# Building the down projection's compact weights in their final layout, and leaving the last batch's outermost two moment sums to TensorE

## The chip, the cores and the metric

The kernel runs on one NeuronCore of a Trainium2 chip. The metric is the device time of one execution in microseconds (us), as a median of several executions; lower is better.

## What is computed

The input `x` has four batches of 512 tokens by 512 features. It is normalised (layer norm without gain), and two branches work on the normalised `xn`: causal attention with 16 heads of width 32 and an ALiBi bias, and a gated feed-forward block whose three weight matrices are not given as matrices but as lists of control points of a cubic (Catmull-Rom) spline.

```python
xn = layernorm(x)
w_gate, w_up = spline(gate_cp).reshape(2048, 512), spline(up_cp).reshape(2048, 512)
w_down = spline(down_cp).reshape(512, 2048)
inter = silu(xn @ w_gate.T) * (xn @ w_up.T)
out = x + attention(xn) + inter @ w_down.T
# spline: sample t lies between control points 1 and 2 of four neighbours p0..p3, at fraction f;
# its weight is a cubic in f with coefficients made of p0..p3
```

One control point covers about 129 samples, so a row of a weight matrix (512 or 2048 samples) hangs on few control points. All data are float32.

## The kernel before, in words

**Attention** is cut into 64 units: batch b, group of four heads, tile of 128 queries. Unit n computes the scores of its tile on TensorE (L847), adds the bias and finds the row extreme on VectorE (L860), takes the exponential on ScalarE (L876), the reciprocal of the sum on VectorE (L889) and the product with it on GpSimd (L891). Three units later TensorE turns the probabilities by products with an identity matrix (L904), and the PSUM result is copied out by ScalarE (L909) or VectorE (L907). Every fourth unit multiplies by the values (L918). Between these steps each unit has a list `items[n]`: projections to q, k, v (L789, L820), the output projection of an earlier batch (L459), sums called moments (L487), loads. Loads and stores are all issued by one engine, SyncE (SP), in program order. The order of every engine's instructions is that of the program text, since `in_order` ties each instruction to the one before it on its engine. So an engine that waits holds back all that stands behind.

The turned tiles, the projections and the moments share one PSUM pool, `ps_m`, with three buffers named `mm`; a new tile can be written only when the copy out of the third tile before it is done.

**Making the weights.** While attention runs, VectorE also makes the feed-forward weights from control points, in small steps taken from a queue called `weights`. Each unit has a budget (2.4, 2.4, 1.2, 2.4 by n modulo 4, less 0.6 for each other small step), spent half in the middle and half at the end of the unit; each step has a cost and the queue is drained until the half is used up. First come the steps for gate and up (`row_weight_steps`, L612 and L615, 128x1024 elements an instruction, tables loaded into the tile `feat[0]` that the feed-forward block needs only later). Behind them comes `down_steps`:

- GpSimd clears the tile `wd` (L636).
- For each of four row groups r and each of 20 control points c, VectorE adds `table[r, c] * point[r, c]` to the columns of `wd` that this point can touch (L652, 80 instructions, 0.6 of the budget each). The point is one number a partition. Two points share a load of `tab` from HBM (L642, two buffers, 40 loads).
- In this form the 128 partitions are output rows. The feed-forward products need the strips the other way round, so TensorE turns `wd` by products with the identity (L668: nine strips of values for each r; L683: the moments), into `ps_m`, and ScalarE copies the result to `dRM` (L675, L684). `dRM` holds `dR`, the values of 9 x 128, and `dM`, the moments of 4 x 128.

**Feed-forward.** For each batch, gate and up products (L1072), Silu (L1087), their product (L1094), and down in two parts: the values (L1168) and the moments. For these, sums of 512-wide rows are formed per eighth e (L1119), copied, and added up from both sides, step by step, by VectorE (L1149, L1150); the results `u[0]` to `u[7]` enter a last product with `dM` (L1183). `down_moments` runs rows r = 3, 2, 1, 0; row 0 takes the outermost sums `u[7]` and `u[0]`, which are the last to be added. Then VectorE adds the residual (L1188) and SP stores the rows (L1189). For the last batch this chain ends the program.

Of the kernel before, what the change touches and what calls it, by code (L numbers as in the profile page):

```python
# [12 lines left out]
F32 = mybir.dt.float32  # L13
# [5 lines left out]
P = 128  # L19
# [25 lines left out]
ND = 64  # L45
NE = 8
NX = 9 + 4
NW, NW4 = 11, 4
NST = NW4 + 1

LINKS = [(0, 0), (2, 1), (1, 0), (2, 2), (1, 1), (3, 2), (4, 3), (3, 3)]
# [195 lines left out]
def down_tables(groups, eighth, alone, order):  # L247
# [75 lines left out]
    rows = np.stack([np.concatenate([groups[NE - 1 - r], groups[r]]) for r in range(NB)])  # L323
    table, ranges = [], []
    for c in range(NCD):
        a = parts[rows, c]
        hit = np.nonzero(a.any(axis=(0, 1, 2)))[0]
        lo, hi = int(hit[0]), int(hit[-1]) + 1
        ranges.append((lo, hi))
        table.append(a[..., lo:hi].reshape(NB, P, -1))  # L330
    return basis, np.concatenate(table, axis=2), ranges, points[rows], rows, homes

# [9 lines left out]
def single(a):  # L342
# [5 lines left out]
_coef, _stretch, ROW_POINTS = row_tables(ORDER)  # L348
_basis, _down, DOWN_RANGES, DOWN_POINTS, _rows, ALONE = down_tables(
    _groups, _eighth, _alone, KEPT  # L350
)
HORDER = _rows.reshape(-1)
# [23 lines left out]
def block_kernel(  # L376
# [45 lines left out]
    basist = keep.tile([P, NRT, ND], F32, name="basist")  # L422
    dpt = keep.tile([P, NB, NCD], F32, name="dpt")
    stretcht = keep.tile([P, len(LINKS), NRT * 4], F32, name="stretcht")
# [17 lines left out]
    dist = wp.tile([P, S], F32, name="dist")  # L442

    wd = wp.tile([P, NB * S], F32, name="wd")
    wdr = wd[:, : NB * NX * Q32].rearrange("p (r t x) -> p r t x", r=NB, x=Q32)
    ctxT = {}
# [79 lines left out]
    with ExitStack() as att:  # L526
        spl = att.enter_context(tc.tile_pool(name="spl", bufs=2))
        attw = att.enter_context(tc.tile_pool(name="attw", bufs=1))
# [26 lines left out]
        load_w("k", Wkp, attw)  # L555
        nc.sync.dma_start(out=dpt, in_=downpts)
        nc.sync.dma_start(out=stretcht, in_=stretch)
# [69 lines left out]

        offsets = np.cumsum([0] + [NX * (hi - lo) for lo, hi in DOWN_RANGES])
        PER = 2
        widest = int(max(offsets[c + PER] - offsets[c] for c in range(0, NCD, PER)))  # L630

        def down_steps():
            tabs = {}

            def clear():
                nc.gpsimd.memset(wd, 0.0)  # L636

            def load(r, c):
                def go():
                    lo, hi = int(offsets[c]), int(offsets[c + PER])  # L640
                    tabs[r, c] = spl.tile([P, widest], F32, name="tab")
                    nc.sync.dma_start(out=tabs[r, c][:, : hi - lo], in_=downtab[r, :, lo:hi])  # L642

                return go

            def term(r, c):
                def go():
                    tab = tabs[r, c - c % PER]
                    at = int(offsets[c] - offsets[c - c % PER])
                    lo, hi = DOWN_RANGES[c]  # L650
                    w = wdr[:, r, :, lo:hi]
                    nc.vector.scalar_tensor_tensor(  # L652
                        w,
                        tab[:, at : at + NX * (hi - lo)].rearrange("p (t x) -> p t x", t=NX),
                        dpt[:, r, c : c + 1],
                        w,
                        ALU.mult,
                        ALU.add,
                    )

                return go

            def turn_values(pairs):
                def go():
                    ps = ps_m.tile([P, NB, P], F32, name="mm")
                    for k, a in enumerate(pairs):
                        for r in range(NB):
                            nc.tensor.matmul(  # L668
                                ps[r * Q32 : (r + 1) * Q32, k, :],
                                lhsT=wdr[:, r, a],  # L670
                                rhs=ident,
                                start=True,
                                stop=True,
                            )
                    nc.scalar.copy(dR[:, pairs[0] : pairs[-1] + 1], ps[:, : len(pairs)])  # L675

                return go

            def turn_moments():
                ps = ps_m.tile([P, NB, P], F32, name="mm")  # L680
                for r in range(NB):
                    m = wdr[:, r, NRT // 2 + 1 :].rearrange("p t x -> p (t x)")
                    nc.tensor.matmul(ps[:, r, :], lhsT=m, rhs=ident, start=True, stop=True)  # L683
                nc.scalar.copy(dM, ps)  # L684

            loads = [(r, c) for r in range(NB) for c in range(0, NCD, PER)]
            steps = [(0.0, clear), (0.0, load(*loads[0])), (0.0, load(*loads[1]))]
            for n, (r, c0) in enumerate(loads):
                steps += [(0.6, term(r, c)) for c in range(c0, c0 + PER)]
                if n + 2 < len(loads):  # L690
                    steps.append((0.0, load(*loads[n + 2])))
            steps += [(1.0, turn_values(range(a, min(a + NB, 9)))) for a in range(0, 9, NB)]
            return steps + [(1.0, turn_moments)]


# [384 lines left out]

    around = {}
    acts, inner, own, sums, res = {}, {}, {}, {}, {}
# [27 lines left out]
    def inner_moments(b, tiles, pool, tag):  # L1110
# [65 lines left out]
    def down_moments(b):  # L1176
# [3 lines left out]
        for r in reversed(range(NB)):  # L1180
            for half, e in ((0, NE - 1 - r), (1, r)):
                cols = slice(half * ND, (half + 1) * ND)
                nc.tensor.matmul(  # L1183
                    sums[b][r][cols, :], lhsT=dM[:, r, cols], rhs=u[e], start=False, stop=True
                )
        for r in reversed(range(NB)):
# [100 lines left out]
```

## Time and profile before

| | before |
|---|---|
| median of 3 runs | 579.06 us (576.9 to 579.31) |
| profiled execution | 578.99 us, span from first to last instruction 576.9 us |
| TensorE busy | 564.1 us (98% of the span) |
| VectorE busy | 373.0 us (65%) |
| ScalarE busy | 296.9 us (51%) |
| GpSimd busy | 184.1 us (32%) |
| mean granted TensorE clock | 0.998 |
| DMA | 69.44 MB, mean 120 GB/s |

The span is what the trace covers; the time of the execution contains 2.1 us more around it. Line numbers (L652) are those of the kernel before. "PE" is TensorE's matmuls, "PEld" its weight loads, DVE is VectorE, ACT is ScalarE, POOL is GpSimd, SP is SyncE and SPq its queue of DMA issues. The trace shows each float32 matmul as two instructions (two passes).

### The profile page before, as it was taken

The numbers are of one execution on the slowest core, as the hardware profiler recorded it, in microseconds if no ns is written. First come the engines' busy times: TensorE is split into PE (matmuls) and PEld (weight loads), VectorE is DVE, ScalarE is ACT, GpSimd is POOL, SyncE is SP. The second block draws the span as 40 slices with busy tenths as digits, with TensorE's granted clock in tenths as the row PEclk, the third lists the DMA queues.
The fourth block names the chain that finished last, engine by engine and source line by source line (L and its number), as shares of the span: only waits on it lengthen the run. The fifth ranks groups of instructions, "written<-read, shape, count | busy, mean of one in ns | idle before, by whom it ended". The sixth has DMA issues, their size and how long they took to land.

```text
span 576.9 us, 11461 instructions
## 1 busy us (share of the span) xinstructions
PE 564.1 (98%) x4088; PEld 279.0 (48%) x4088; DVE 373.0 (65%) x1047; ACT 296.9 (51%) x786; POOL 184.1 (32%) x333
## 2 busy tenths in 40 slices
PE   7999999999999999999999999999999999999996
PEld 5645555444445555454555555555535333343342
DVE  6169988877687777768675444556244673854737
ACT  2457666554456665645655576677514512623322
POOL 2034525334232424233243242443124133122310
PEclk9999999999999999999999999999999999999999
DMA  8932246312422623432241004602445576774334
GB/s 310 337 70 74 73 148 219 95 25 60 152 81 73 212 69 106 114 122 65 68 142 46 2 1 97 124 1 84 137 129 175 107 175 197 135 203 171 112 149 159
DMA packets 36216, 69.44 MB, mean 120 GB/s; under 512 B 5984, under 2 KB 9568, under 8 KB 35648
## 3 DMA queue, kind: packets, MB, share of 16 engines
q1 hardware_dynamic: 36160, 68.72, 41.4%
q8 instruction: 32, 0.52, 0.4%
q14 instruction: 24, 0.20, 0.1%
HBM read 44.06 MB, written 15.29 MB: 103 GB/s over the span
## 4 chain that ended last, share of the span: by engine, by line
PE 76%; DMA 7%; DVE 7%; ACT 5%; SPq 3%; issue 1%; POOL 0%; DVEq 0%; POOLq 0%
PE mm L789 18%; PE mm L904 11%; PE mm L820 10%; PE s L847 6%; PE mm L459 6%; PE g L1072 6%; PE c L918 4%; PE o L1168 3%; ACT p L876 3%; PE o L459 3%; DMA feat<-samples 2%; PE o L1119 2%; PE mm L487 2%; DVE p L860 2%; PE g L1119 1%; PE o L1183 1%
## 5 line engine op out<-in xcount | busy, mean ns | idle before, releaser
L891 POOL TENSOR_SCALAR p<-p,inv 128x128 f32<-128x128 f32 (+3 forms) x256 | 140.2, 567 | 261.0 <-DVE inv L889 217.8
L876 ACT ACTIVATE p<-p,low 128x128 f32<-128x128 f32 (+3 forms) x256 | 140.7, 553 | 48.8 <-DVE low L860 48.5
L860 DVE CUSTOM_DVE_ANT_0 p<-s,dist 128x128 f32<-128x128 f32 (+3 forms) x256 | 109.1, 482 | 31.7 <-PE s L847 31.3
L904 PEld LDWEIGHTS mm<-ident,p 128*128 128x128 f32 x640 | 71.1, 141 | 40.6 <-issue 26.5
L904 PE MATMUL mm<-ident,p 128*128 128x128 f32 x640 | 89.2, 278 | 1.2 <-ACT pT L909 0.7
L909 ACT COPY pT<-mm 128x512 f32<-128x512 f32 x96 | 55.2, 580 | 53.4 <-PE mm L904 53.0
L1095 POOL COPY made<-inner 128x512 f32<-128x512 f32 x64 | 38.8, 633 | 109.6 <-DVE inner L1094 84.2
L1087 ACT ACTIVATE act<-g 128x512 f32<-128x512 f32 x64 | 33.3, 603 | 62.5 <-PE g L1072 62.5
L1072 PE MATMUL g<-feat,wT 32*128 32x512 f32 x432 | 59.6, 612 | 0.8 <-DMA feat<-moments 0.6
L820 PE MATMUL mm<-wv,xnT 128*128 128x512 f32 x128 | 58.3, 597 | 1.6 <-DMA wv<-in_Wvp_dram 1.0
L789 PE MATMUL mm<-xnT,wk 128*128 128x512 f32 (+1 forms) x136 | 59.3, 579 | 0.2 <-ACT xnT L774 0.2
L789 PE MATMUL mm<-xnT,wq 128*128 128x512 f32 (+1 forms) x136 | 58.0, 569 | 0.3 <-ACT pT L909 0.2
L847 PE MATMUL s<-kT,qT 32*128 32x512 f32 (+3 forms) x512 | 51.3, 468 | 0.3
L1094 DVE TENSOR_TENSOR inner<-g,act 128x512 f32<-128x512 f32 x44 | 27.3, 684 | 33.5 <-issue 10.1
L876 ACT ACTIVATION_READ_ACCUMULATOR p<-p,low 128x1 f32 x256 | 48.5, 189 | 0.0
L907 DVE COPY pT<-mm 128x512 f32<-128x512 f32 x64 | 43.6, 686 | 4.8 <-PE mm L904 4.2
L652 DVE SCALAR_TENSOR_TENSOR wd<-tab,dpt,wd 128x260 f32<-128x260 f32 (+7 forms) x80 | 39.8, 497 | 7.9 <-DMA tab<-in_downtab_dram 3.5
L1072 PEld LDWEIGHTS g<-feat,wT 32*128 32x128 f32 x432 | 23.7, 184 | 34.0 <-issue 19.1
L459 PE MATMUL mm<-ctxT,wo 128*128 128x512 f32 x88 | 40.0, 597 | 0.0
L918 PE MATMUL c<-pT,v 128*32 128x128 f32 (+3 forms) x512 | 37.8, 436 | 0.0
L789 PEld LDWEIGHTS mm<-xnT,wk 128*128 128x128 f32 x136 | 24.5, 189 | 25.2 <-issue 21.9
L789 PEld LDWEIGHTS mm<-xnT,wq 128*128 128x128 f32 x136 | 24.7, 190 | 23.3 <-issue 22.1
(103 smaller groups left out, 565.3 us busy)
## 6 DMA issues: line engine op xcount, KB each, us to landing
inner<-made SPq DMA_DIRECT2D x32, 256.0 KB
feat<-samples SPq DMA_DIRECT2D x64, 88.0 KB
xp<-in_xp_dram SPq DMA_DIRECT2D x16, 256.0 KB
samples<-xnT SPq DMA_DIRECT2D x4, 1024.0 KB
feat<-in_coef_dram SPq DMA_DIRECT2D x8, 512.0 KB
feat<-in_rowpts_dram SPq DMA_DIRECT2D x32, 128.0 KB
xt<-in_xT_dram SPq DMA_DIRECT2D x16, 256.0 KB
mid<-xt SPq DMA_DIRECT2D x16, 256.0 KB
```

The lines of the kernel that those rows point to most:

```text
L459: nc.tensor.matmul(ps, lhsT=wsb["o"][:, c, r * P : (r + 1) * P], rhs=ctxT[b][:, c, :], start=(c == 0), stop=(c == NB - 1),)
L789: nc.tensor.matmul(ps[0][:, tokens], lhsT=wsb[name][:, c, hg * P : (hg + 1) * P], rhs=xnT[b][:, c, tokens], start=(c == 0), stop=(c == NB ...
L820: nc.tensor.matmul(ps[0], lhsT=xnT[b][:, c, t * P : (t + 1) * P], rhs=wsb["v"][:, c, :], start=(c == 0), stop=(c == NB - 1),)
L847: nc.tensor.matmul(banks[b, hg][j][:, at : at + (k + 1) * P], lhsT=qk[b, hg, "q"][rows, k * P : (k + 1) * P], rhs=qk[b, hg, "k"][rows, : ( ...
L860: nc.vector.tensor_tensor_reduce(out=p[:, j, :nk], in0=ps[j], in1=dist[:, S - nk :], scale=-SLOPES[hg * NG + j], scalar=BIG, op0=ALU.add, ...
L876: nc.scalar.activation(p[:, j, :nk], p[:, j, :nk], AF.Exp, bias=low[:, j : j + 1], scale=-1.0, accum_out=total[:, j : j + 1],)
L891: nc.gpsimd.tensor_scalar(p[:, j, :nk], p[:, j, :nk], inv[:, j : j + 1], 1.0, ALU.mult, ALU.mult)
L904: nc.tensor.transpose(ps[:, j, :], p[:, j, c * P : (c + 1) * P], ident)
L907: nc.vector.tensor_copy(out, ps)
L909: nc.scalar.copy(out, ps)
L918: nc.tensor.matmul(ps[j * HD : (j + 1) * HD, c * P :], lhsT=vals[b][:, c, hg * P + j * HD : hg * P + (j + 1) * HD], rhs=w[:, j, :], start= ...
L1072: nc.tensor.matmul(ps[k], lhsT=wT[rows, q, 2 * w + part, :], rhs=feat[b][rows, part, q, :], start=(part == 0), stop=(part == 1),)
```

## The change

The host now arranges, for every element of the strips in their final layout, the few control points that this element depends on: five for values, four for moments. Two arrays of equal shape go to the chip: `downtab` (coefficients) and `downpts` (the control point for each coefficient). Fourteen steps remain: values 0 to 4 of the nine, five steps of 128x640; values 5 to 8, five of 128x512; moments, four of 128x512. A step multiplies the two arrays element by element and adds the product to `dR` or `dM` in place (the first of each group writes there directly), so 25 VectorE instructions in all, each with 0.9 of the budget. There are 28 loads, two for a step, three steps in flight, into `feat[0]`, where the tables of the gate and up steps were; products go through `wd`. The clearing of `wd`, the turning by TensorE and the four copies by ScalarE are gone, as is the `tab` pool and the load of `dpt`.

For the last batch, the two outermost sums are not formed: `u[0]` becomes the pair (`u[1]`, `turned[1]`) and `u[7]` the pair (`u[6]`, `turned[1]`), and row 0 of the last product is two matmuls accumulated in place of one, for each half.

```diff
 def down_steps():
-    (clear wd; 40 loads of tab; 80 x term; turn_values; turn_moments)
+    size = 5 * P
+    spare = feat[0].rearrange("p h c s -> p (h c s)")
...
+    def load(n):
+        def go():
+            at, width = given[n]
+            for k, source in enumerate((downtab, downpts)):
+                to = spare[:, (n % 3 * 2 + k) * size :][:, :width]
+                part = source[at : at + P * width].rearrange("(p x) -> p x", p=P)
+                nc.sync.dma_start(out=to, in_=part)
...
+        def times():
+            nc.vector.tensor_tensor(tmp, tab, own, ALU.mult)
+        def plus():
+            nc.vector.tensor_tensor(to, to, tmp, ALU.add)
+        return [times, plus] if c else [times]
+
+    steps = [(0.0, load(n)) for n in range(3)]
+    for n in range(len(DOWN_STEPS)):
+        steps += [(0.9, half) for half in term(n)]
+        if n + 3 < len(DOWN_STEPS):
+            steps.append((0.0, load(n + 3)))
+    return steps
...
 def inner_moments(b, tiles, pool, tag):
...
+            if b == B - 1:
+                parts.pop()
+                u[0], u[-1] = [u[1], turned[:, 1]], [u[-2], turned[:, 1]]
...
 def add_moments(b, n):
-        if len(steps) == NE - 2:
+        if not turning[b]:
+            turning[b] = True
...
 def down_moments(b):
...
-                nc.tensor.matmul(
-                    sums[b][r][cols, :], lhsT=dM[:, r, cols], rhs=u[e], start=False, stop=True
-                )
+                parts = u[e] if isinstance(u[e], list) else [u[e]]
+                for k, part in enumerate(parts):
+                    nc.tensor.matmul(
+                        sums[b][r][cols, :],
+                        lhsT=dM[:, r, cols],
+                        rhs=part,
+                        start=False,
+                        stop=(k == len(parts) - 1),
+                    )
```

More of the change, by code (lines that the diff above doesn't have):

```diff
@@ L46 @@
 NE = 8
+NCV = 5
 NX = 9 + 4
@@ L49 @@
 NST = NW4 + 1
+DOWN_STEPS = [("v", lo, hi, c) for lo, hi in ((0, 5), (5, 9)) for c in range(NCV)]
+DOWN_STEPS += [("m", 0, NB, c) for c in range(4)]
 LINKS = [(0, 0), (2, 1), (1, 0), (2, 2), (1, 1), (3, 2), (4, 3), (3, 3)]
@@ L323, in down_tables, with own_points @@
     rows = np.stack([np.concatenate([groups[NE - 1 - r], groups[r]]) for r in range(NB)])
[L324 to L331, printed above, removed]
+    table, numbers = own_points(parts[rows], points[rows])
+    return basis, table, numbers, rows, homes
+def own_points(parts, points):
+    values = parts[:, :, :, :9].transpose(0, 4, 3, 1, 2)
+    values = values.reshape(P, 9, 2, P // 2, NCD)
+    moments = parts[:, :, :, 9:].transpose(3, 4, 0, 1, 2)
+    moments = moments.reshape(P, NB, 2, P // 2, NCD)
+    strip = np.broadcast_to(points[:, None, None], (NB, Q32, 9, P, NCD)).reshape(values.shape)
+    group = np.broadcast_to(points[None], (P, NB, P, NCD)).reshape(moments.shape)
+    own = {}
+    for kind, a, number, n in (("v", values, strip, NCV), ("m", moments, group, 4)):
+        hit = (a != 0.0).any(axis=3)
+        first = np.where(hit.any(axis=3), hit.argmax(axis=3), 0)
+        first = np.minimum(first, NCD - n)[:, :, :, None, None] + np.arange(n)
+        first = np.broadcast_to(first, (*a.shape[:4], n))
+        few = np.take_along_axis(a, first, axis=4)
+        assert np.count_nonzero(few) == np.count_nonzero(a)
+        shape = (*a.shape[:2], P, n)
+        own[kind] = few.reshape(shape), np.take_along_axis(number, first, axis=4).reshape(shape)
+    steps = [[a[:, lo:hi, :, c].reshape(-1) for a in own[k]] for k, lo, hi, c in DOWN_STEPS]
+    return *(np.concatenate(a) for a in zip(*steps)),
 def query_scales():
@@ L348 @@
 _coef, _stretch, ROW_POINTS = row_tables(ORDER)
-_basis, _down, DOWN_RANGES, DOWN_POINTS, _rows, ALONE = down_tables(
-    _groups, _eighth, _alone, KEPT
-)
+_basis, _down, DOWN_POINTS, _rows, ALONE = down_tables(_groups, _eighth, _alone, KEPT)
 HORDER = _rows.reshape(-1)
@@ L422, in block_kernel @@
     basist = keep.tile([P, NRT, ND], F32, name="basist")
-    dpt = keep.tile([P, NB, NCD], F32, name="dpt")
     stretcht = keep.tile([P, len(LINKS), NRT * 4], F32, name="stretcht")
@@ L444, in block_kernel @@
     wd = wp.tile([P, NB * S], F32, name="wd")
-    wdr = wd[:, : NB * NX * Q32].rearrange("p (r t x) -> p r t x", r=NB, x=Q32)
     ctxT = {}
@@ L526, in block_kernel @@
     with ExitStack() as att:
-        spl = att.enter_context(tc.tile_pool(name="spl", bufs=2))
         attw = att.enter_context(tc.tile_pool(name="attw", bufs=1))
@@ L555, in block_kernel @@
         load_w("k", Wkp, attw)
-        nc.sync.dma_start(out=dpt, in_=downpts)
         nc.sync.dma_start(out=stretcht, in_=stretch)
@@ L625, in row_weight_steps @@
             return steps
-        offsets = np.cumsum([0] + [NX * (hi - lo) for lo, hi in DOWN_RANGES])
-        PER = 2
-        widest = int(max(offsets[c + PER] - offsets[c] for c in range(0, NCD, PER)))
         def down_steps():
[L633 to L638, printed above, removed]
-                def go():
-                    lo, hi = int(offsets[c]), int(offsets[c + PER])
-                    tabs[r, c] = spl.tile([P, widest], F32, name="tab")
-                    nc.sync.dma_start(out=tabs[r, c][:, : hi - lo], in_=downtab[r, :, lo:hi])
-                return go
[L646 to L693, printed above, removed]
@@ new lines, in down_steps @@
+            size = 5 * P
+            spare = feat[0].rearrange("p h c s -> p (h c s)")
+            given, at = [], 0
+            for _, lo, hi, _ in DOWN_STEPS:
+                given.append((at, (hi - lo) * P))
+                at += P * (hi - lo) * P
+            def load(n):
+                def go():
+                    at, width = given[n]
[3 more added lines that the diff above has]
+                        nc.sync.dma_start(out=to, in_=part)
+                return go
@@ new lines, in term @@
+            def term(n):
+                kind, lo, hi, c = DOWN_STEPS[n]
+                width = given[n][1]
+                to = (dR if kind == "v" else dM)[:, lo:hi].rearrange("p a n -> p (a n)")
+                tmp = wd[:, n % 2 * size :][:, :width] if c else to
+                tab, own = (spare[:, (n % 3 * 2 + k) * size :][:, :width] for k in range(2))
+                def times():
[3 more added lines that the diff above has]
+                return [times, plus] if c else [times]
@@ L1079, in product @@
         return ps
-    around = {}
+    around, turning = {}, [False] * B
     acts, inner, own, sums, res = {}, {}, {}, {}, {}
@@ L1182, in down_moments @@
                 cols = slice(half * ND, (half + 1) * ND)
-                nc.tensor.matmul(
-                    sums[b][r][cols, :], lhsT=dM[:, r, cols], rhs=u[e], start=False, stop=True
-                )
+                parts = u[e] if isinstance(u[e], list) else [u[e]]
[7 more added lines that the diff above has]
+                    )
         for r in reversed(range(NB)):
@@ L1264 @@
     given["rowpts"] = np.ascontiguousarray(rows)
-    given["downpts"] = np.ascontiguousarray(down[DOWN_POINTS].transpose(1, 0, 2))
+    given["downpts"] = np.ascontiguousarray(down[DOWN_POINTS])
     given["coef"], given["stretch"], given["basis"] = COEF, STRETCH, BASIS
```

## The prediction

> **What bounds the kernel now.** I read the busy table first, then TensorE in stretches, then the groups of the lines that change, then the order of time around the two places where TensorE's own work changes.
>
> ```profile
> PE 564.1 (98%) x4088; PEld 279.0 (48%) x4088; DVE 373.0 (65%) x1047; ACT 296.9 (51%) x786; POOL 184.1 (32%) x333
> ```
>
> TensorE is busy 98% of the span. That alone doesn't prove that it is the limit in every stage, so the table by stretches comes next (start:end and length, then busy us of PE, PEld, DVE, ACT, POOL, each with its instructions; then granted clock, DMA share, GB/s).
>
> ```profile
> 138.00:165.00 27.00, 26.85 (x103) 12.31 (x104) 17.87 (x67) 11.83 (x35) 9.32 (x16) 1.00 0.28 92
> 165.00:200.00 35.00, 35.00 (x228) 18.90 (x227) 26.09 (x88) 21.43 (x63) 12.11 (x23) 1.00 0.42 126
> 300.00:345.00 45.00, 44.43 (x316) 23.59 (x314) 22.86 (x80) 27.56 (x77) 15.86 (x32) 1.00 0.12 41
> 550.00:577.00 27.00, 21.85 (x308) 10.18 (x301) 14.58 (x22) 7.33 (x13) 2.35 (x4) 0.96 0.44 158
> ```
>
> Where Down's weights are made (143 to 321 us) TensorE has no gap worth the name, at full clock, and no other engine is busy for more than about three quarters of these stretches. Only at the end (550 to 577) does it idle for 5 us; there a chain of VectorE adds and the last stores set the time. So instructions taken off TensorE should shorten the run by their own length; VectorE's savings count for nothing unless VectorE makes TensorE wait.
>
> **The part on TensorE: the turning goes.** These groups vanish (busy us, mean ns of one; idle before them and its releaser):
>
> ```profile
> L668 PE MATMUL mm<-ident,wd 128*32 128x128 f32 x72 | 2.6, 277 | 0.0
> L683 PE MATMUL mm<-ident,wd 128*128 128x128 f32 x8 | 1.2, 288 | 0.0
> L652 DVE SCALAR_TENSOR_TENSOR wd<-tab,dpt,wd 128x260 f32<-128x260 f32 (+7 forms) x80 | 39.8, 497 | 7.9 <-DMA tab<-in_downtab_dram 3.5 <-POOL wd L636 3.1
> ```
>
> Means mislead here, because the 32-column products overlap. I take the time from one start to the next in TensorE's timeline:
>
> ```profile
> 308.13 1.08 PE L668 MATMUL mm<-ident,wd 128*32 128x128 f32 x32
> 309.14 3.70 PE L820 MATMUL mm<-wv,xnT 128*128 128x512 f32 x8
> ...
> 313.65 1.08 PE L668 MATMUL mm<-ident,wd 128*32 128x128 f32 x32
> 314.66 1.14 PE L847 MATMUL s<-kT,qT 32*128 32x512 f32 x8
> ...
> 318.61 0.43 PE L668 MATMUL mm<-ident,wd 128*32 128x128 f32 x8
> 318.96 1.16 PE L683 MATMUL mm<-ident,wd 128*128 128x128 f32 x8
> 320.69 3.70 PE L820 MATMUL mm<-wv,xnT 128*128 128x512 f32 x8 [0.57 <-ACT pT L909]
> ```
>
> 309.14 - 308.13 = 1.01, 314.66 - 313.65 = 1.01, and 320.69 - 318.61 = 2.08, of which 0.57 is a wait for a buffer of `ps_m`. That wait goes too: of the pool's last three tiles one is then the one turned at 312.7, copied out at 313.3, instead of the one whose copy stood behind four exponentials until 320.64. Sum: 4.10 us. Does anything else come late then? ScalarE has 27.56 of 45 us there and loses four copies (2.0 us), VectorE has 22.86 of 45 and idles 6 us before its copy at 324.43. So I count all 4.10.
>
> **The part on VectorE: fewer, wider, earlier.** 80 instructions, 39.8 us, become 25. A 128x1024 product from SBUF (L612) takes 1.214 us and a 64x512 sum (L1149) 0.684; between them 128x640 is about 0.82. Sum: 9 x 0.82 + 16 x 0.684 = 18.3 us, 21.5 less. The 3.1 us wait for GpSimd's clearing at 140 goes as well. I count this at nothing: TensorE was busy 35.00 of 35.00 us beside it. But it isn't harmless, because the work is bunched. In the instruction order of the new kernel all 25 lie in ten units, the span from 140 to about 205 in the old times, against 140 to 306. Mostly a unit's share falls (two of 0.82 for four of 0.48). Three consecutive units, those starting at 187.9, 195.5 and 199.5, get four of 0.684, or 2.74 us, for 2.0 to 2.2 us. The last two are short, 4.0 and 4.8 us, and VectorE is nearly full in them.
>
> **The loads.** Their bytes fall, from 9.66 MB (40 loads, by the sizes in the table of DMA issues) to 2 x 14 arrays of 128x640 or 128x512, 8.0 MB. They move into `feat[0]`; the first three steps wait for the last gate and up product, which ends at 136.75, and SP has nothing else to issue between 132.7 and 144.8. Their first user, at about 140, reads the pair that is free to go at 131.8. The tight spot is later. SP in the old run:
>
> ```profile
> 188.42 1.85 SPq L545 DMA_DIRECT2D xp<-in_xp_dram  x4
> 191.44 4.50 SPq L642 DMA_DIRECT2D tab<-in_downtab_dram  x2
> 196.00 0.43 SPq L474 DMA_DIRECT2D samples<-xnT  x1
> ```
>
> In the new order the 1 MB of `xp` is followed by the loads of steps 10 and 11, then the 1 MB of `samples`, then the loads of steps 12 and 13, each of 0.52 MB. A load waits for the product three steps before it, so step 11 can be asked for at 195.6 and is wanted at 198.8. In the old run the 0.23 MB load issued at about 195.6 held VectorE 0.51 us at 198.63, so it took about 3.0 us; 0.29 MB more at 0.3 to 0.4 MB/us makes about 4 us: 1 us late. Steps 12 and 13, behind `samples`, may be late by 0.5 to 1 us each. Together VectorE runs 2 to 3 us later by 204 than before. Behind these instructions stand the reductions L860, which free the score banks, and the copies L907, which free `ps_m`. What such a delay costs TensorE the old trace shows:
>
> ```profile
> 129.98 0.68 DVE L502 COPY out<-mm 64x512 f32<-64x512 f32 x1 [3.10 <-DMA moments<-out]
> ...
> 149.44 0.68 DVE L502 COPY out<-mm 64x512 f32<-64x512 f32 x1 [4.08 <-DMA moments<-out]
> ```
>
> VectorE stood still 3.10, 3.14 and 4.08 us in 27 us, and TensorE lost 0.8 us between 100 and 138 and 0.15 between 138 and 165. Bounds for the bunching: 0 (all hidden; even -0.3, for the short waits that go) and 3 (all of it on TensorE). I take 0.4, near the row that it resembles.
>
> The load of `dpt` leaves SP's start, behind the weights that the start waits for: nothing.
>
> **The end of the program.** VectorE's timeline (and one line of TensorE's) before:
>
> ```profile
> 569.67 0.68 DVE L1149 TENSOR_TENSOR edge<-xp,xnT 64x512 f32<-64x512 f32 x1
> ...
> 570.38 0.69 DVE L1150 TENSOR_TENSOR edge<-ctxT,xnT 64x512 f32<-64x512 f32 x1
> 571.10 2.48 DVE L1188 TENSOR_TENSOR res<-o,res 128x512 f32<-128x512 f32 x4
> ...
> 571.13 1.08 PE L1183 MATMUL o<-edge,dRM 128*64 128x512 f32 x4 [0.36 <-DVE edge L1150]
> ```
>
> Two adds go, 1.43 us, and the first three residual sums move up by that. The fourth now waits for TensorE: row 1 starts at 569.7, a pass takes 0.43 to 0.48, and row 0 has four matmuls of two passes, in two halves of the array. If the halves run side by side, row 0 ends four passes after 570.6, at 572.5, and the last residual sum at 573.2 against 573.58: 0.4 gained. If the second half starts only when the first one's second matmul has, it is six passes: 0.5 lost. Three of the four stores also go 1.4 us sooner, so the last has the DMA engines for itself, worth up to 0.7 more (4 x 0.26 MB at the 410 GB/s seen at the end last 2.6 us). Range -1.1 to +0.5; I take -0.3, nearer to side by side, because in the old trace the two halves' passes of one row start within 0.01 us of each other (568.76 and 568.77).
>
> The Trainium skill (TensorE: Matmul & The Clock Gate, "Step-by-step: what each phase is for") says that matmuls keep program order and only weight loads are pulled ahead. Taken strictly that rule speaks against this edit: the second half's matmuls stand behind both of the first, the tail would be +0.5, and the sum would be 575.8 instead of 575.0. The row with both halves starting together doesn't settle it, since there no matmul stands behind another of its own half.
>
> **Sum.** 578.99 (the profiled execution, span 576.9 plus 2.1) - 4.10 + 0.4 - 0.3 = 575.0 us. The profiled execution is 0.07 below the median of the runs, so this stands for the median too.
>
> **Rivals.** First, no measurable change: the bunched loads cost 2 to 3 us, or the softmax chain takes the place of the turning, since the chain of waits passes exponentials at 316.66. Against it: TensorE waits for it only the 0.57 that I counted. Price: 4.1 - 3 - 0 leaves 1 us, 577 to 579. Second, slower: the three-deep loads don't keep up, and steps 10 to 13 each wait for a full landing of some 4.4 us (the 3.0 above for 0.23 MB, the rest by bytes, 0.4 for the second issue) between 196 and 204. That is 17 us of standstill; less the 4 us that a standstill was seen to cost nothing, 13 us on TensorE, and 578.99 - 4.4 + 13 = 587.6; if half of it overlaps, some 582. It decides the sign once more than 8 us aren't hidden. For it: DMA moved 212 GB/s in the slice at 187 to 202 in the old run and SP issues in order; against it: two of these four loads are asked for a whole unit ahead. Third, the tail alone loses 0.5 and nothing else differs: 575.8, inside my case.
>
> **Numbers.** My case, 574 to 576.1: 0.64. No change by measure (0.5% is 2.9 us, about what a measurement of this kernel can tell from none; so down to 576.2 and up to 582): 0.24. Slower: 0.12. Low end: 4.1 + 1.1 + 0.3 of gain is 573.5, and runs of the kernel before scatter by some 2 us downward; 573.2. High end: 3 us of standstill and 0.5 at the tail give 578.4, and a part of the second rival; 578.8.
>
> **What would show it.** In the new profile: no L668 and L683 group, TensorE's instructions down by 80 and up by 4; VectorE near 351 us; TensorE between 300 and 345 without the 0.57 wait; waits of VectorE for `feat` from `in_downtab` or `in_downpts` of 1 to 4 us in sum around 195 to 205, and TensorE still without a gap of 1 us there; at the end the last residual sum within 0.5 us of two adds earlier or level. I am wrong if VectorE waits over 8 us for these loads, if TensorE shows new gaps after 140 of more than 2 us in sum, or if ScalarE becomes what TensorE waits for between 308 and 345.

## The result, and the profile after

The changed kernel takes 575.84 us (median of 22 runs, 572.45 to 579.76) against 580.0 us (22 runs, 576.9 to 584.2) for the kernel before on the same chips: ratio 0.9934, 95% interval 0.9915 to 0.9954. That is 4.2 us less (2.7 to 4.9), where 4.0 were forecast; the forecast time was 575.0 us (573.2 to 578.8). The profiled execution took 573.35 us, with a span of 571.6.

The line numbers of the new kernel differ: the products and sums that make the weights are L668 and L671, the turning of the probabilities is L891 (before L904), the projection L807 (L820), the scores L834 (L847), the adds of moments L1142 and the residual L1186. The busy table of the changed kernel:

```profile
PE 560.7 (98%) x4012; PEld 276.7 (48%) x4012; DVE 355.3 (62%) x990; ACT 295.8 (52%) x782; POOL 184.8 (32%) x332
```

TensorE has 76 instructions fewer (80 gone, 4 new) and VectorE is busy 17.7 us less. The prediction's sums gave 21.5 for the weights and 1.4 for the two adds. The groups do fall by 20.6 (39.8 to 19.2), but successive instructions of VectorE overlap in the trace, so that a sum of their means counts some time twice. In the stretches of the changed kernel (columns as in the prediction):

```profile
138.00:165.00 27.00, 26.18 (x108) 12.33 (x105) 18.91 (x62) 12.13 (x36) 6.78 (x13) 1.00 0.54 159
165.00:200.00 35.00, 35.00 (x224) 18.59 (x223) 26.91 (x83) 22.31 (x64) 13.83 (x23) 1.00 0.45 146
300.00:345.00 45.00, 45.00 (x266) 23.52 (x265) 21.47 (x83) 29.06 (x86) 17.50 (x34) 1.00 0.02 7
```

Between 300 and 345 the 0.57 us gap is gone: 45.00 of 45.00. The 0.82 us without work between 138 and 165 (0.15 before) is no new loss: 0.67 of it is a wait for ScalarE at 139.34, which stands at 137.92 before, just outside the stretch. VectorE is a little busier than before in the two stretches in which it now makes the weights (18.91 and 26.91 us for 17.87 and 26.09), DMA moves more (159 and 146 GB/s for 92 and 126), and TensorE's 35.00 of 35.00 stays. The new groups of the changed kernel (busy us, mean ns of one; idle before and its releaser):

```profile
L668 DVE TENSOR_TENSOR wd<-feat 128x512 f32<-128x512 f32 (+1 forms) x11 | 8.5, 770 | 0.3 <-DMA feat<-in_downpts_dram 0.2
L671 DVE TENSOR_TENSOR dRM<-dRM,wd 128x512 f32<-128x512 f32 (+1 forms) x11 | 8.5, 769 | 0.1
L668 DVE TENSOR_TENSOR dRM<-feat 128x512 f32<-128x512 f32 (+1 forms) x3 | 2.2, 727 | 0.0
```

19.2 us in 25 instructions, with almost no waiting before them.

**Where the time went.** The start and the feed-forward stage differ between any two executions by a few us, so the two spans alone can't place the gain. I took the same TensorE products as landmarks in every profile: the second block of products with `wq` (17.4 us in the kernel before), two projections to q on either side of the stretch where the turning stood (297.7 and 326.1), the last output projection (430.7) and the last batch's first moments (552.0). The next table, worked out from TensorE's timelines, has each landmark's start minus its start in the kernel before. The last column is the length of the tail: from the start of the tenth add of moments, which both versions have, to the end of the span; spans are printed to 0.1 us, so it is good to 0.05.

| kernel | 17.4 | 297.7 | 326.1 | 430.7 | 552.0 | tail, us |
|---|---|---|---|---|---|---|
| before | 0 | 0 | 0 | 0 | 0 | 7.95 |
| after | +1.42 | +1.40 | -3.09 | -3.59 | -4.25 | 7.28 |
| changed_again (same kernel) | +0.54 | +0.52 | -3.97 | -4.48 | -4.30 | 7.26 |
| down_only | +2.84 | +2.82 | -1.67 | -2.18 | +0.88 | 7.87 |
| tail_only | +2.99 | +2.98 | +2.98 | +2.48 | +2.71 | 7.51 |
| new_sums_still_turned | +1.15 | +1.14 | +1.12 | +0.61 | +2.59 | 7.91 |
| old_sums_not_turned | +2.51 | +2.53 | -1.97 | -2.48 | -1.97 | 7.89 |
| one_step_in_flight | +1.00 | +10.97 | +6.48 | +5.98 | +5.60 | 7.28 |
| two_steps_in_flight | +2.73 | +2.72 | -1.77 | -2.27 | -0.13 | 7.28 |
| turned_part_first | +2.93 | +2.91 | -1.58 | -2.08 | +0.01 | 7.14 |
| feat_halves_together | -0.27 | -0.27 | -4.77 | -5.28 | +1.46 | 7.27 |
| res_then_feat_first | +4.24 | +4.22 | -0.27 | -0.77 | -0.17 | 7.12 |

Read it by differences of neighbouring columns. The first column comes from the start of the program, above all from the wait for the load of `wv`: 1.0 us in the profile of before, none in feat_halves_together and 1.1 to 2.7 in the others, those with the old sums too. It is no property of the change. Between 17.4 and 297.7, where the new sums lie, the changed kernel loses and gains nothing (1.40 - 1.42). Between 297.7 and 326.1 it gains 4.49. The 0.5 of the next column is in every profile, that of the unturned and of the turned kernels alike, so it belongs to the one profile of before. From 430.7 to 552.0 the differences scatter from -0.7 to +6.7; more on that below. From 552.0 to the tenth add is a last stretch, 16.95 us before, 16.57 after and 16.54 to 17.35 in the others, which also differs within one kind of kernel. The tail is 0.67 shorter.

TensorE's timeline in the changed kernel, where the turning was:

```profile
308.51 1.09 PE L891 MATMUL mm<-ident,p 128*128 128x128 f32 x8
309.44 3.60 PE L807 MATMUL mm<-wv,xnT 128*128 128x512 f32 x8
312.88 1.04 PE L891 MATMUL mm<-ident,p 128*128 128x128 f32 x8
...
317.21 0.66 PE L891 MATMUL mm<-ident,p 128*128 128x128 f32 x4
317.70 3.60 PE L807 MATMUL mm<-wv,xnT 128*128 128x512 f32 x8
321.23 0.94 PE L834 MATMUL s<-kT,qT 32*128 32x128 f32 x16
```

The step from one start to the next tells more than the groups. A block of eight instructions that turn probabilities lasts 309.44 - 308.51 = 0.93 us here; in the kernel before, with the 32-column turning behind them, they last 1.02 (307.11 to 308.13). The projection lasts 3.44 and 3.53 us here, 3.54 and 3.63 before; the block of four 0.49, 0.59 before. So four neighbours of the removed blocks each became 0.10 us shorter: 0.39 on top of the 4.10 that the starts of the blocks themselves gave. Together that is the 4.49 of the landmarks.

The Trainium skill (TensorEngine Tiling (Array Packing), "Key Properties") says that changing the tiling mode drains the array. The trace fits that at three of the four places, where the removed 32-column products stood next to 128-column ones: 0.09 to 0.10 us each. The fourth is the projection at 320.69, whose first product came late by the same 0.10; it stood behind 128-column products and the wait of 0.57, so no change of tile explains it. That the time at the other three is a drain was not tested.

### The profile page after: what moved, and what is told of

The parts are those of the page before. It is cut to its first block, busy times and chain, and to the rows that moved or that the text cites. A ratio compares the mean times of both kernels' runs of the same rounds, so it can differ in the third digit from the quotient of the medians.

```text
span 571.6 us, 11202 instructions
## 1 busy us (share of the span) xinstructions
PE 560.7 (98%) x4012; PEld 276.7 (48%) x4012; DVE 355.3 (62%) x990; ACT 295.8 (52%) x782; POOL 184.8 (32%) x332
## 4 chain that ended last, share of the span: by engine, by line
PE 87%; DVE 5%; ACT 4%; DMA 3%; issue 1%; SPq 1%; DVEq 0%
PE mm L776 18%; PE mm L891 11%; PE mm L807 10%; PE g L1059 9%; PE mm L475 7%; PE s L834 7%; PE o L1160 6%; PE c L905 5%; PE o L1106 3%; PE o L1177 3%; PE o L475 3%; ACT p L863 2%; PE mm L503 2%; PE o L1059 2%; DMA wv<-in_Wvp_dram 1%; DVE p L847 1%
## 5 line engine op out<-in xcount | busy, mean ns | idle before, releaser
L878 POOL TENSOR_SCALAR p<-p,inv 128x128 f32<-128x128 f32 (+3 forms) x256 | 142.5, 576 | 257.0 <-DVE inv L876 246.8
L847 DVE CUSTOM_DVE_ANT_0 p<-s,dist 128x128 f32<-128x128 f32 (+3 forms) x256 | 109.2, 482 | 36.2 <-PE s L834 35.3
L891 PEld LDWEIGHTS mm<-ident,p 128*128 128x128 f32 x640 | 71.0, 141 | 40.4 <-issue 25.5
L891 PE MATMUL mm<-ident,p 128*128 128x128 f32 x640 | 89.0, 278 | 1.2 <-ACT pT L896 0.7
L807 PE MATMUL mm<-wv,xnT 128*128 128x512 f32 x128 | 58.1, 595 | 2.3 <-DMA wv<-in_Wvp_dram 2.3
L1059 PE MATMUL g<-feat,wT 32*128 32x512 f32 x432 | 57.9, 611 | 0.0
L834 PE MATMUL s<-kT,qT 32*128 32x512 f32 (+3 forms) x512 | 51.1, 468 | 0.3
L894 DVE COPY pT<-mm 128x512 f32<-128x512 f32 x64 | 43.6, 687 | 9.1 <-PE mm L891 8.6
L807 PEld LDWEIGHTS mm<-wv,xnT 128*128 128x128 f32 x128 | 23.0, 190 | 26.1 <-issue 26.0
```

Of the source, the lines that this page charges most:

```text
L807: nc.tensor.matmul(ps[0], lhsT=xnT[b][:, c, t * P : (t + 1) * P], rhs=wsb["v"][:, c, :], start=(c == 0), stop=(c == NB - 1),)
L834: nc.tensor.matmul(banks[b, hg][j][:, at : at + (k + 1) * P], lhsT=qk[b, hg, "q"][rows, k * P : (k + 1) * P], rhs=qk[b, hg, "k"][rows, : ( ...
L847: nc.vector.tensor_tensor_reduce(out=p[:, j, :nk], in0=ps[j], in1=dist[:, S - nk :], scale=-SLOPES[hg * NG + j], scalar=BIG, op0=ALU.add, ...
L878: nc.gpsimd.tensor_scalar(p[:, j, :nk], p[:, j, :nk], inv[:, j : j + 1], 1.0, ALU.mult, ALU.mult)
L891: nc.tensor.transpose(ps[:, j, :], p[:, j, c * P : (c + 1) * P], ident)
L894: nc.vector.tensor_copy(out, ps)
```

## The experiments

Ratios are to the kernel before, measured beside it in the same job (medians of before 580.1 to 580.4 us there).

**One part without the other.** The first takes the new sums and leaves the tail as before; the second is the kernel before with the new tail alone.

```diff
 # down_only: the changed kernel
-            if b == B - 1:
+            if b == B:
                 parts.pop()
 # tail_only: the kernel before
+            if b == B - 1:
+                parts.pop()
+                u[0], u[-1] = [u[1], turned[:, 1]], [u[-2], turned[:, 1]]
 (and row 0 with two matmuls for each half, as in the change)
```

> The change without its second part: the last batch's outermost two sums are formed by VectorE as before. Theory (the time goes where TensorE loses its 80 turning matmuls): 4.1 to 4.3 us faster than before, ratio about 0.9928, and the last residual sum again 1.4 us after the last two adds. Rival (the end of the program brings most): only 1 to 3 us faster, ratio above 0.995.

> The kernel before with the second part alone: row 0 of the last product gets two matmuls for each half, VectorE two adds less. Theory: 0.3 to 0.7 us faster, ratio 0.9988 to 0.9995, which timing alone can hardly tell from 1; in the profile the two halves of row 0 run side by side, about 1.9 us for the four passes, and VectorE waits about 1 us for TensorE ahead of its last residual sum. Rival (matmuls keep program order across halves): six passes or more, 2.7 us and up, and the end 0.5 us later than before.

Measured: down_only 0.994 (0.9914 to 0.9966), tail_only 1.0007 (0.9981 to 1.0032). So nearly all of the gain is that of the new sums. The tail's part, some 0.45 us in its own profile (7.51 against 7.95), is too small for the runs to tell. It is seen only in the landmarks: 7.87 to 7.95 us in the four profiles with the old tail, 7.26 to 7.51 in the six others with the tail of the change, and 7.12 and 7.14 in the two that reorder it.

**Is it the turning or the sums?** The third kernel makes the weights in the new way, and still runs the old turning on TensorE and its copies on ScalarE, on data that nobody reads, at the old place. The fourth is the kernel before without the turning: its compact weights stay zero, so the down projection's share is left out of the output, with every product on it still done.

```diff
 # new_sums_still_turned: down_only, and
+        items[46].insert(0, turn_again(range(0, 4)))
+            small[46].append(turn_again(range(4, 8)))
+        items[47].insert(0, turn_moments_again)
+        items[47].insert(0, turn_again(range(8, 9)))
 # old_sums_not_turned: the kernel before, and
+        nc.gpsimd.memset(dRM, 0.0)
-            steps += [(1.0, turn_values(range(a, min(a + NB, 9)))) for a in range(0, 9, NB)]
-            return steps + [(1.0, turn_moments)]
+            return steps
```

> VectorE makes the weights in the new way and they are used, but TensorE still does 80 identity matmuls at the old places, on the leftover contents of wd, and ScalarE copies them to a scratch tile that nobody reads; the end as before. Theory: the gain is gone, 578.5 to 580, ratio 0.999 to 1.001, and TensorE again waits some 0.5 us for ScalarE's copy at about 320. Rival (VectorE's 21 us less, or the wait for the clearing that went, bring the gain): stays at 0.993 to 0.996.

> The kernel before without the turning and its four copies; dR and dM are zeros from a GpSimd memset at the start, so down's part is left out of the output, with every product on it still done. Theory: as fast as the change's first part, ratio about 0.993, although VectorE still has its 80 instructions; TensorE's stretch from 308 to 321 shorter by 4.1. Rival (bunching costs the new sums something): this one is faster than down_only by 0.4 us or more; rival (VectorE's relief helps): slower than down_only by over 1 us. Zero weights could also make the chip run cooler, so the granted clock must be the same for the comparison to count.

Measured: new_sums_still_turned 1.0037 (1.0014 to 1.006), old_sums_not_turned 0.993 (0.9892 to 0.9968). Old sums without the turning gain as much as the whole change; new sums with the turning gain nothing. The mean granted clock of the runs was 0.9957 with the zero weights and 0.9950 before, near enough for the comparison to count. Their stretches from 300 to 345, first new sums and turning, then old sums without it:

```profile
300.00:345.00 45.00, 44.45 (x316) 23.86 (x315) 19.84 (x73) 28.25 (x81) 14.54 (x30) 1.00 0.02 6
```

```profile
300.00:345.00 45.00, 45.00 (x269) 23.63 (x268) 26.16 (x99) 29.11 (x84) 19.62 (x36) 1.00 0.15 48
```

With the turning TensorE has its 316 instructions and its short gap back, although VectorE is less busy there than ever (19.84). Without it the gap is gone, although VectorE still adds up the old way (26.16). In TensorE's waits of the kernel with the turning stands the wait that the prediction counted at 0.57:

```profile
PE g L1089 <- DMA feat<-moments: 1.5, 2, 1.3
...
PE mm L833 <- ACT pT L922: 0.6, 1, 0.6
```

Between 297.7 and 326.1 the landmarks move by -0.02 us in this kernel and by -4.50 in the other. The rival that bunching costs the new sums something finds no support: old_sums_not_turned has the lower median by 1.0 us, but the intervals overlap and the clock of down_only was lower (0.9933); between 17.4 and 297.7 the landmarks move by +0.02 there and by -0.02 in down_only. So the 18 us that VectorE saves are worth nothing by themselves; the layout that makes the turning needless is what pays.

That new_sums_still_turned is slower than the kernel before, by 2.1 us, wasn't expected. Its first line above is part of the answer, and the last section takes it up.

**What late loads would cost.** The prediction feared 2 to 3 us of lateness, and its second rival 17 us of standstill. These two kernels keep the loads of one or two steps in flight in place of three.

```diff
-            steps = [(0.0, load(n)) for n in range(3)]
+            steps = [(0.0, load(n)) for n in range(1)]      # two_steps_in_flight: range(2)
...
-                if n + 3 < len(DOWN_STEPS):
-                    steps.append((0.0, load(n + 3)))
+                if n + 1 < len(DOWN_STEPS):                 # two_steps_in_flight: n + 2
+                    steps.append((0.0, load(n + 1)))
```

> The changed kernel with one step's two loads in flight instead of three, so that VectorE waits for a landing before nearly every one of 13 steps. It prices the standstill that the second rival spoke of. Theory: some 4 us of wait a step, 40 to 55 us in sum, in units of 4 to 8 us with one or two steps each; TensorE, which hides about 4 us in a unit, comes 10 to 25 us late by the time of 300 us, and the run is 585 to 600 us. Rival (VectorE has so much room that TensorE hides it): less than 3 us late.

> The changed kernel with two steps in flight instead of three. Theory: VectorE waits 1 to 2 us for some of the steps, 5 to 12 us in sum, mostly between 190 and 210; TensorE's products stand where they stood in the changed kernel within 0.5 us, so a standstill of this size costs nothing. Rival (VectorE is nearly full there, so that every us shows): TensorE 3 us or more later by 300 us than by 138.

Measured, one run each: 583.96 and 577.46 us, before 580.08. With one step in flight VectorE waits 15.0 us for these loads, in five waits, where 40 to 55 us were expected before nearly every step. Two of the waits in VectorE's timeline of that kernel (the bracket is the idle time before the instruction and what ended it):

```profile
154.35 0.82 DVE L668 TENSOR_TENSOR wd<-feat 128x640 f32<-128x640 f32 x1 [3.91 <-DMA feat<-in_downpts_dram]
...
164.52 0.83 DVE L668 TENSOR_TENSOR wd<-feat 128x640 f32<-128x640 f32 x1 [4.83 <-DMA feat<-in_downpts_dram]
```

and what they do to TensorE, in its timeline and in the stretches after each:

```profile
157.27 0.66 PE L891 MATMUL mm<-ident,p 128*128 128x128 f32 x4 [1.98 <-DVE pT L894]
...
167.98 0.66 PE L891 MATMUL mm<-ident,p 128*128 128x128 f32 x4 [2.67 <-DVE pT L894]
```

```profile
158.00:160.00 2.00, 2.00 (x12) 1.08 (x13) 1.51 (x7) 0.73 (x2) 0.00 (x0) 0.57 0.27 102
...
170.00:172.00 2.00, 2.00 (x6) 0.84 (x3) 1.86 (x9) 0.47 (x1) 0.93 (x2) 0.52 0.07 26
```

VectorE's waits hold back its copies L894 of turned probabilities, TensorE runs out of `ps_m` buffers some 3 us later, stands 1.98 and 2.67 us, and then gets half its clock for a while: 0.57 and 0.52 of it in the two stretches shown. All in all 10 us are lost by landmark 297.7. That is the low end of the 10 to 25 that were expected, and the run is under its 585. The rival's mechanism is real, then, and its price is by no means the length of the standstill less a fixed 4 us: 15.0 us of waiting cost 10. Nor does each wait cost its length: the one of 4.02 us at 181.60 was followed by a wait of TensorE of only 0.51. With two steps in flight one wait of 0.8 us is left, where 5 to 12 us in sum were expected, and TensorE loses nothing (+2.73 and +2.72). Three steps are enough, and two nearly so.

**The tail's order.** The product of row 0 with `turned[1]` needs no add, so it can go ahead of all rows. This kernel issues it there.

```diff
+        if isinstance(u[0], list):
+            for half, e in ((0, NE - 1), (1, 0)):
+                cols = slice(half * ND, (half + 1) * ND)
+                nc.tensor.matmul(sums[b][0][cols, :], lhsT=dM[:, 0, cols],
+                                 rhs=u[e].pop(), start=False, stop=False)
         (the loop over the rows 3, 2, 1, 0)
```

> The changed kernel with row 0's two products with the turned sums issued ahead of row 3, when they are ready long before, and not last. Theory (in the tail TensorE is back to back from the last values to row 0, so order doesn't matter): the last residual sum comes at the same distance from the first of the four rows' products within 0.15 us, after correcting for the 0.9 us that the early products take. Rival (row 0 waits in line for its own halves): the last residual sum 0.5 to 0.9 us earlier.

Measured: one run, 577.45 us; tail 7.14 us against 7.28. The last residual sum ends 4.15 us after the tenth add in place of 4.31. TensorE has the same products in front of that sum whatever their order, and it is busy from the first of those moved (567.47) to the end of the last at 571.98 without a gap. Its last product and VectorE's last residual sums:

```profile
571.39 0.59 PE L1187 MATMUL o<-xp,dRM 128*64 128x512 f32 x1
```

```profile
570.31 0.69 DVE L1196 TENSOR_TENSOR res<-o,res 128x512 f32<-128x512 f32 x1 [0.17 <-PE o L1187]
571.17 0.69 DVE L1196 TENSOR_TENSOR res<-o,res 128x512 f32<-128x512 f32 x1 [0.17 <-PE o L1187]
572.02 0.69 DVE L1196 TENSOR_TENSOR res<-o,res 128x512 f32<-128x512 f32 x1 [0.17 <-PE o L1187]
```

Each residual sum now waits 0.17 us for its row, and they follow each other at TensorE's pace of two passes a row, 0.86 us. The tail gets 0.14 shorter. The order of these products matters little: the tail now ends when TensorE has done them all.

**The feed-forward stage, two attempts to improve on the change.** Several profiles show TensorE waiting in this stage for `feat`, which is loaded in two halves (F0, F1 in the written order of each batch). The first kernel moves the second half next to the first; the second also moves the load of the residual rows (L) ahead of both, and has the tail's order from above.

```diff
 # feat_halves_together (batch 0 in the first line)
-        "F0 G0 P0 U0 F1 P1 G1 P2 U1 P3 G2 V2 G3 V3",
-        "F0 G0 m0:8 U0 L F1 m8:16 G1 T R0:6 ...",
+        "F0 F1 G0 P0 U0 P1 G1 P2 U1 P3 G2 V2 G3 V3",
+        "F0 F1 G0 m0:8 U0 L m8:16 G1 T R0:6 ...",
 # res_then_feat_first
+        "L F0 F1 G0 m0:8 U0 m8:16 G1 T R0:6 ...",
```

> The changed kernel with the second half of the next batch's feature loads issued with the first half at the start of each feed-forward batch, not after its first quarter. It tests whether the gaps of TensorE ahead of a batch's first gate products (waits of 0.6 to 1.9 us for the moments' features, after which the granted clock falls for some us) make the scatter from run to run. Theory: these waits are gone, the stretch from the last output projection to the last batch's moments takes 120.5 to 121 us, the median falls by 1 to 3 us against the changed kernel (ratio to before 0.988 to 0.992) and the runs lie closer together. Rival (DMA is full, so earlier loads only push back others): within 1 us of the changed kernel.

> The changed kernel with three moves of order: at the start of each feed-forward batch the residual's load comes first, then both halves of the next batch's features (before: first half, and residual and second half after the first quarter), and row 0's products with the turned sums come ahead of row 3. Theory: with the residual's load no longer behind the features, neither TensorE's wait for the residual sum (5.9 us in the run with the halves together) nor the wait for the moments' features is left, the granted clock stays at 1.00 through the feed-forward stage, the stretch from the last output projection to the last batch's moments takes 120.5 to 121.5 us, and the median is 572 to 574 us, ratio to before 0.986 to 0.990. Rival (DMA is full in that stage, so one transfer or another comes late in any order): within 1 us of the changed kernel or slower.

Measured: feat_halves_together 1.0106 (1.0061 to 1.0151); res_then_feat_first 0.9953 (0.9923 to 0.9984), beside the changed kernel again, in the same job, at 0.9927 (0.9897 to 0.9956). In the first the waits for `feat` are gone, but the load of the residual now comes late (it is issued at 468.50, after 459.69 in the changed kernel), the residual sums with it, and TensorE waits for the buffer that they free. VectorE's wait, the longest line in TensorE's waits, and the stretch:

```profile
475.02 2.48 DVE L1186 TENSOR_TENSOR res<-o,res 128x512 f32<-128x512 f32 x4 [8.04 <-DMA res<-mid]
```

```profile
PE o L1059 <- DVE res L1186: 7.2, 2, 5.9
```

```profile
460.00:480.00 20.00, 14.08 (x113) 7.13 (x101) 7.08 (x12) 3.78 (x8) 2.29 (x4) 0.80 0.81 222
```

DMA is busy at 0.81 there: what one load gains another loses. The second kernel has neither of these waits. A wait for `inner` behind them, 0.3 us in the changed kernel and 0.8 in its repeat, has become 2.2, also with a lower clock:

```profile
PE o L1106 <- DMA inner<-made: 2.2, 1, 2.2
```

```profile
480.00:500.00 20.00, 17.84 (x218) 6.25 (x210) 8.49 (x13) 6.78 (x13) 4.63 (x8) 0.91 0.59 192
```

Its interval overlaps that of the changed kernel, and its median is 1.6 us higher. My theory that an earlier load of `feat` makes the stage faster fell twice; no version was found that beats the change.

> The changed kernel unaltered, on the same chip as the run beside it, for a direct comparison and for a second profile of it. Theory: ratio to before 0.992 to 0.9945; in the profile TensorE's products after the place of the turning stand 4.5 us earlier, measured from the start offset of the run, and the end 7.3 us behind the tenth add. Rival (the gain is an accident of one profile): ratio within 0.998 to 1.002.

Measured: 575.74 us, ratio 0.9927, inside the expected range. Its landmarks move by -4.49 between 297.7 and 326.1, and its tail is 7.26 us, so the profile of the change was no accident.

## Why the prediction was right

**The turning, -4.10 predicted, -4.49 measured.** The removed blocks, taken from start to start, were right to the hundredth, and so was the wait of 0.57 as one that disappears with its cause. The 0.39 that was missing lies in the neighbours, 0.10 in each of four, which no start-to-start step of the block itself shows: three next to a change of tile, one behind the wait.

**VectorE's bunching, +0.4 predicted, 0.00 measured.** The sums took 19.2 us where 18.3 were estimated, because a few ran longer than the 0.69 and 0.82 us of most (the one at 201.46 below took 1.09). The term that was mis-sized is what lateness of the loads costs TensorE, and in this profile the lateness itself. The 0.4 was taken near a row that doesn't price it: 0.67 of the 0.8 us that TensorE lost between 100 and 138 is one wait for ScalarE's copy L909 (at 137.92), and no run ties it to VectorE's standstill. VectorE and SP in the changed kernel at the place where 1 us and twice 0.5 to 1 us of lateness were expected:

```profile
201.46 1.09 DVE L668 TENSOR_TENSOR wd<-feat 128x512 f32<-128x512 f32 x1
...
205.43 0.69 DVE L668 TENSOR_TENSOR wd<-feat 128x512 f32<-128x512 f32 x1 [0.24 <-DMA feat<-in_downpts_dram]
```

```profile
197.02 0.33 SPq L656 DMA_DIRECT2D feat<-in_downtab_dram  x1
197.40 0.43 SPq L656 DMA_DIRECT2D feat<-in_downpts_dram  x1
197.93 0.38 SPq L490 DMA_DIRECT2D samples<-xnT  x1
199.86 0.36 SPq L656 DMA_DIRECT2D feat<-in_downtab_dram  x1
```

The loads issued at 197.0 and 197.4 (195.6 and 196.0 on the clock of before, whose landmarks lie 1.4 us earlier) are used at 201.46 without a wait. So 4 us from issue to use were enough, as estimated; it was the user that came at 200.1 on the old clock and not at 198.8. The steps behind the 1 MB of `samples` together waited 0.24 us in place of 1 to 2. In the second profile of the same kernel the same step waited longer, near the forecast:

```profile
205.53 0.69 DVE L668 TENSOR_TENSOR wd<-feat 128x512 f32<-128x512 f32 x1 [1.23 <-DMA feat<-in_downpts_dram]
```

The landmarks say that TensorE noticed neither (-0.02 us in both profiles). It was right, on the other hand, that late loads were the danger: the kernel with one step in flight shows it, though at 157 and 168 us and not at 195 to 205.

**The tail, -0.3 predicted (-1.1 to +0.5), -0.67 measured.** VectorE's timeline in the changed kernel, and TensorE's last products:

```profile
564.32 0.69 DVE L1142 TENSOR_TENSOR ctxT<-ctxT,xnT 64x512 f32<-64x512 f32 x1
565.04 1.89 DVE L1186 TENSOR_TENSOR res<-o,res 128x512 f32<-128x512 f32 x3
567.94 0.69 DVE L1186 TENSOR_TENSOR res<-o,res 128x512 f32<-128x512 f32 x1 [1.02 <-PE o L1177]
```

```profile
565.97 0.59 PE L1177 MATMUL o<-ctxT,dRM 128*64 128x512 f32 x1
565.98 0.64 PE L1177 MATMUL o<-xp,dRM 128*64 128x512 f32 x1
566.40 0.59 PE L1177 MATMUL o<-ctxT,dRM 128*64 128x512 f32 x1
566.46 0.59 PE L1177 MATMUL o<-xp,dRM 128*64 128x512 f32 x1
566.83 1.08 PE L1177 MATMUL o<-xnT,dRM 128*64 128x512 f32 x4
```

The last residual sum waits 1.02 us for TensorE, as forecast: the two adds of 1.43 us bring only 0.32 (it ends 4.31 us after the tenth add begins, before 4.63). Another 0.35 lies behind it, where the last store now runs without the three others. The prediction priced that at up to 0.7 and left it out of its value. That the stores are the reason is not shown: in tail_only, whose stores move up in the same way, this part is only about 0.15 shorter.

The program issues row 0 as `u[6]` (`ctxT`), `turned[1]`, `u[1]` (`xp`), `turned[1]`, and the trace shows `ctxT` and `xp` together at 565.97 and 565.98 and both products with `turned[1]` (in `xnT`) behind them. The two halves run side by side, four passes in 1.94 us.

The Trainium skill's rule that matmuls keep program order (TensorE: Matmul & The Clock Gate, "Step-by-step: what each phase is for") would have put `xp` behind the first product with `turned[1]`, six passes in all. For two matmuls in different column halves of the array this trace doesn't show the order of the program text, and the measurement decides. Whether the compiled program or the chip put `xp` ahead, the trace doesn't tell.

**The sum.** Landmarks give -4.49 + 0.00 - 0.67 = -5.2 us. One more term was taken as unchanged: an execution lasts 2.1 us longer than its span before and 1.8 after (2.12 and 1.79 as means of the runs). It goes with the new sums (1.8 in down_only, 2.1 in tail_only); the reason was not sought. So the parts make -5.5. The medians give -4.2, with -4.9 as the end of their interval. That 4.0 was forecast and 4.2 measured is therefore partly luck: each term came out better than forecast, and some 1.3 us of that don't show in the medians. The stretch that differs most between profiles is the feed-forward stage, whose length (from landmark 430.7 to 552.0) is 121.35 us in the profile of before and 120.7 to 124.4 in the nine other profiles whose kernels leave its written order alone: 121.4 to 121.9 in the three with the old sums, 120.7 to 124.4 with a mean of 122.5 in the seven with the new. Whether the new sums make this stage about 1 us longer, or so few profiles scatter that way, these runs can't tell; that stays open.

**The rivals.** The first (no measurable change, from 2 to 3 us of lateness or from the softmax chain) fell with the landings: the waits were 0.24 and 1.23 us, without a loss on TensorE, and where the turning stood TensorE is busy 45.00 of 45.00 us. The second (standstill) has its mechanism shown in one_step_in_flight, but the changed kernel is far from it. The third, half a us lost at the tail, was wrong in sign.

## What to carry to other kernels

Where one engine is busy 98% of the span, price an edit by that engine's starts, from the instruction before the removed block to the instruction after it, and count both neighbours too. Work saved on the other engines is worth what it takes off the waits of the first one, here nothing, and work that is bunched there costs nothing as long as its loads come in time. In a stage that keeps both TensorE and DMA busy (DMA 0.81 where it was looked at) an earlier load need not pay: in the two orders tried here the wait moved to another load, and the sum was level or worse.

## What the runs showed of the hardware

**A short gap can be followed by half a clock, and its length alone doesn't decide.** new_sums_still_turned waits 1.28 us for `feat` at 515 and then shows these stretches:

```profile
514.00:516.00 2.00, 1.02 (x6) 0.19 (x2) 2.00 (x4) 0.00 (x0) 0.00 (x0) 1.00 0.93 166
...
518.00:520.00 2.00, 2.00 (x6) 1.03 (x6) 0.00 (x0) 0.40 (x1) 0.00 (x0) 0.50 0.89 316
...
524.00:526.00 2.00, 2.00 (x44) 0.64 (x32) 0.00 (x0) 0.00 (x0) 0.00 (x0) 1.00 0.72 263
```

The granted clock falls to 0.50 and is back at 1.00 after 524. The same kernel as the change, run again, waits 0.69 us at the same place and keeps its clock:

```profile
512.00:514.00 2.00, 1.31 (x7) 0.41 (x5) 0.91 (x2) 0.60 (x1) 0.00 (x0) 1.00 0.90 175
514.00:516.00 2.00, 2.00 (x28) 0.74 (x34) 0.00 (x0) 1.57 (x3) 0.12 (x1) 1.00 0.77 276
```

turned_part_first waits as long there, 0.70 us, and loses it:

```profile
516.03 1.96 PE L1059 MATMUL g<-feat,wT 32*128 32x512 f32 x6 [0.70 <-DMA feat<-moments]
```

```profile
514.00:516.00 2.00, 1.32 (x5) 0.29 (x2) 1.58 (x3) 0.60 (x1) 0.00 (x0) 1.00 1.01 132
...
518.00:520.00 2.00, 2.00 (x24) 0.78 (x32) 0.00 (x0) 0.76 (x2) 1.09 (x2) 0.59 0.65 235
```

And feat_halves_together waits 1.26 us at 515.43 and keeps 1.00 through 526. So a gap of 0.7 us can cost more than itself, and a longer one nothing; what decides, these profiles don't show. In the runs, time goes with the mean granted clock: the correlation is -0.83 over the 22 runs of the changed kernel and -0.69 to -0.96 in the other sets of several runs. A straight line through time against clock gives, as an estimate for a clock of 1, 577.3 us before, 573.5 for the change (572.5 when it was run again), 575.0 for down_only, 577.1 for new_sums_still_turned and 573.3 for old_sums_not_turned. By this estimate new_sums_still_turned is level with the kernel before, and its 2.1 us go with its lower mean clock, 0.9908 against 0.9950. Why its clock is lower more often was not tried; that the gap causes the drop is read from the profiles alone.
